# A cross-attention on one core: GpSimd computes the exponents' offset, and queues it ahead of the last scale broadcast

## The chip, the cores and the metric

The kernel runs on one core of a Trainium2 chip. A core has five engines with an instruction queue each: TensorE (PE in the profile), VectorE (DVE), ScalarE (ACT), GpSimd (POOL) and SyncE (SP), which here only issues DMAs. POOL issues DMAs too. Each queue runs in order, and queues wait for each other by semaphores. The metric is the device time in microseconds (us) of one execution of the whole program.

## The reference

The reference adds three blocks to an input x of 4 x 128 rows of 1024: a cross-attention to a context of 4 x 2048 tokens, a causal self-attention, and a feed-forward block with 4-bit weights. The change lies in the first:

```python
q, k: quantised per row of a head (64 values): q = sq * qi, k = sk * ki   # qi, ki integers
attn = softmax(q @ k.T)                     # over all 8192 tokens of the 4 batches
attn = clip(round(attn / (max(attn)/255)), 0, 255) * (max(attn)/255)
out  = attn @ v                             # v quantised per column
```

A row's largest softmax value is reached at its largest score. With s = (qi @ ki) * sk, the integer that stands for an attention value is therefore round(exp(sq * s - sq * max(s) + log 255)); the softmax's sum is needed only at the end. The offset m = -sq * max(s) + log 255, one number a row, is what this change is about.

## The kernel before

The program has stages in this order: quantised queries; keys and values of all 8192 tokens (to about 1509 us), which go through DRAM; the cross-attention; its output projection, the self-attention and the feed-forward block. The change touches the cross-attention alone.

It works through 64 units: 16 heads h, and in each head 4 row tiles t of 128 rows. A unit has 8 steps g of 1024 tokens. A loop writes out the order of the work by hand, one step after another (L876 and on; nothing reorders it), and what is issued in a step goes to the engines' queues in that order:

- scores (L746): two PE matmuls (L759) into one of two PSUM tiles sc; then DVE (L766) multiplies by the scales sk of the tokens, writes e, and keeps the chunk's largest value in a column of mx. The tile e holds half a unit (4 chunks) and has three buffers.
- maximum (L777), after the unit's eighth chunk: DVE reduces mx to its largest value (L781) and a tensor_scalar makes the offset m of it (L783): m * nsq + log 255, where nsq is -sq.
- exponentials (L789), for the unit before, at steps 0 and 4: ACT reads half a unit of e, with m as the bias, and writes int16 (tile a, three buffers).
- transposes (L803, PE and an ACT copy, 12 steps after the scores) and dma_transposes (L817, issued by SP) turn a; values (L828, PE, 18 steps after) multiplies by v.

In the last unit of a head (t = 3) each step also prepares the next head: load_keys at the first four steps, and spread_scales (L737): a POOL partition_broadcast (L739) copies one row of 1024 scales from sk_row to all 128 partitions of a tile sk. There are 8 such tiles for the 8 steps and as many buffers, so the broadcast of step g can be made only when DVE has used the same tile for the last time, in that very step. After the eighth broadcast load_rows (L731) issues, on POOL, four small DMAs that bring the row of the head after next. load_values (L726) issues the DMAs of v on POOL, four for each pair of heads.

So POOL's queue holds, for a head: eight broadcasts, four row loads and on average two loads of values; the offset m is on DVE.

Of the kernel before, what the change touches and what calls it, by code (L numbers as in the profile page):

```python
# [58 lines left out]
NSC = NK // SC  # L59
# [25 lines left out]
def tile_perceiver(  # L85
# [26 lines left out]
    nc = tc.nc  # L112
# [498 lines left out]
    def load_keys(h, c):  # L611
        kt = pools["keys"].tile([P, KC // 2], BF16, name=f"kt{h}_{c}", tag="kt", bufs=6)
        nc.sync.dma_start(out=kt, in_=k_d[c][h].rearrange("f d n -> (f d) n"))
        kts[h, c] = kt

    def tile_of_scales(h, g):
        sks_at[h, g] = pools["keys"].tile([P, SC], F32, name=f"sk{h}_{g}", tag="sk", bufs=NSC)
        return sks_at[h, g]
# [100 lines left out]
    with tc.tile_pool(name="at_s", bufs=4) as small, tc.tile_pool(  # L719
# [6 lines left out]
        def load_values(p, c):  # L726

            vqs[p, c] = at.tile([P, KT // NKC, P], F16, name=f"vq{p}_{c}", tag="vq", bufs=NKC + 1)
            nc.gpsimd.dma_start(out=vqs[p, c], in_=vq_d[p, :, ts(c, KT // NKC), :])

        def load_rows(h):  # L731

            sks_at[h] = at.tile([P, KC], F32, name=f"sk_row{h}", tag="sk_row", bufs=1)
            for c in range(NKC):
                nc.gpsimd.dma_start(out=sks_at[h][32 * c : 32 * c + 1, :], in_=sk_d[c][h : h + 1, :])

        def spread_scales(h, g):  # L737
            c, half = divmod(g, 2)
            nc.gpsimd.partition_broadcast(  # L739
                tile_of_scales(h, g), sks_at[h][32 * c : 32 * c + 1, ts(half, SC)], channels=P  # L740
            )
# [4 lines left out]
        def scores(n, g):  # L746

            h, t = units[n]
            if g == 0:
                mx = small.tile([P, NSC], F32, name="mx", tag="mx")  # L750
                state[n] = {"mx": mx, "e": [], "a": []}
            if g % (NSC // NEC) == 0:
                e = at.tile([P, EC], F32, name="e", tag="e", bufs=3)
                state[n]["e"].append(e)
            ps = sc_ps.tile([P, SC], F32, name="sc", tag="sc")

            for i in range(2):
                rows = slice(D * i, D * i + D)
                nc.tensor.matmul(  # L759
                    ps[:, ts(i, 512)],  # L760
                    lhsT=qT[rows, h, ts(t, P)],
                    rhs=kts[h, g // 2][rows, ts(g % 2, 512)],
                    start=True,
                    stop=True,
                )
            nc.vector.tensor_tensor_reduce(  # L766
                out=state[n]["e"][-1][:, ts(g % (NSC // NEC), SC)],
                in0=ps,
                in1=sks_at[h, g],
                scale=1.0,  # L770
                scalar=LOWEST,
                op0=ALU.mult,
                op1=ALU.max,
                accum_out=state[n]["mx"][:, g : g + 1],
            )

        def maximum(n):  # L777
            h, t = units[n]
            st = state[n]
            m = st["m"] = small.tile([P, 1], F32, name="m", tag="m")  # L780
            nc.vector.tensor_reduce(m, st["mx"], AX.X, ALU.max)  # L781

            nc.vector.tensor_scalar(  # L783
                m, m, nsq[:, t, h : h + 1], math.log(255.0), ALU.mult, ALU.add
            )
            if t == 0:
                sums[h] = small.tile([P, NT, NEC], F32, name="sum", tag="sum")

        def exponentials(n, c):  # L789
            h, t = units[n]  # L790
            st = state[n]
            a = at.tile([P, EC], I16, name="a", tag="a", bufs=3)
            st["a"].append(a)
            nc.scalar.activation(  # L794
                a,
                st["e"][c],
                AF.Exp,
                bias=st["m"],
                scale=sq[:, t, h : h + 1],
                accum_out=sums[h][:, t, c : c + 1],  # L800
            )

        def transposes(n, g):  # L803

            a = state[n]["a"][g // (NSC // NEC)].bitcast(F32)
            at_word = SC // 2 * (g % (NSC // NEC))
            pt = at_ps.tile([P, SC // 256, P], F32, name="a_pt", tag="a_pt")
            for i in range(SC // 256):
                nc.tensor.transpose(  # L809
                    pt[:, i, :], a[:, at_word + P * i : at_word + P * i + P], ident  # L810
                )
            aT = at.tile([P, SC // 256, P], I32, name="aT", tag="aT", bufs=4)
            nc.scalar.copy(aT, pt.bitcast(I32))
            aT = aT.bitcast(F16).rearrange("p i (q e) -> p i e q", e=2)
            state[n]["aT", g] = [aT[:, i // 2, i % 2, :] for i in range(SC // P)]

        def dma_transposes(n, c):  # L817

            at_key = c * KC % EC
            a = state[n]["a"][c * KC // EC][:, at_key : at_key + KC].bitcast(F16)  # L820
            aT = at.tile([P, KC // P, P], F16, name="aT_d", tag="aT_d", bufs=3)
            nc.sync.dma_start_transpose(out=aT, in_=a)
            for g in range(KC // SC):
                state[n]["aT", KC // SC * c + g] = [
                    aT[:, g * (SC // P) + i, :] for i in range(SC // P)
                ]
# [45 lines left out]
        def at_step(s):  # L872
            return divmod(s, NSC) if 0 <= s < n_steps else None

        with tc.manual_schedule():
            for s in range(n_steps + LAG_V):  # L876
                n, g = divmod(s, NSC)
                if s == 1:
                    for c in range(NKC):
                        load_values(0, c)  # L880
                if g == NSC // NEC and 1 <= n <= len(units):
                    dma_transposes(n - 1, DMA_KC[0])
                if g == 0 and 2 <= n <= len(units) + 1:
                    dma_transposes(n - 2, DMA_KC[1])
                if g % (NSC // NEC) == 0 and 1 <= n <= len(units):
                    exponentials(n - 1, g // (NSC // NEC))
                if n < len(units):
                    h, t = units[n]
                    scores(n, g)
                    if t == NT - 1 and h + 1 < H:  # L890

                        if g < NKC:
                            load_keys(h + 1, g)
                        spread_scales(h + 1, g)
                        if g == NSC - 1 and h + 2 < H:
                            load_rows(h + 2)
                    if g == NSC - 1:
                        maximum(n)
                at_lag = at_step(s - LAG_T)
                if at_lag and at_lag[1] * SC // KC not in DMA_KC:  # L900
                    transposes(*at_lag)
                if at_step(s - LAG_V):
                    values(*at_step(s - LAG_V))

                pair, since = divmod(s - NSC * (2 * NT - 1), NSC * 2 * NT)
                if 0 <= pair < NP - 1 and since in (0, LAG_V + 1, LAG_V + 3, LAG_V + 5):
                    load_values(pair + 1, max(0, since - LAG_V + 1) // 2)
# [290 lines left out]
    with tc.manual_schedule():  # L1198
# [11 lines left out]
        for h, (w, n) in enumerate(PARTS):  # L1210
# [20 lines left out]
            for t in range(NT):  # L1231
                g = s + GROUP * t
# [233 lines left out]
```

## Time and profile before

| | us |
|---|---|
| median of 3 runs (2888.08 to 2891.64) | 2890.35 |
| the profiled execution | 2888.83 |
| its span, first to last instruction | 2887.1 |

| engine | busy us | share of the span |
|---|---|---|
| PE | 2666.1 | 92% |
| DVE | 2411.5 | 84% |
| ACT | 1271.2 | 44% |
| POOL | 444.4 | 15% |

A line of a group of instructions reads: line of the kernel, engine, operation, tile written <- tiles read, shapes, count | busy us in all, mean ns of one | idle time of the engine just before them, with what ended most of it. A line of the timeline reads: start, duration, engine, line, operation, tiles, count, and in brackets the idle time before it and what ended it. A line for a stretch of time reads: start:end and its length, then for PE, PE's weight loads, DVE, ACT and POOL the busy us (and count), then PE's clock, the DMA engines' share and GB/s. An engine's name with a q behind it means the sequencer of that engine, which handles waits and configuration. Spans on POOL are rough.

### The profile page before, as it was taken

Reading aid. Unit: us, or ns where it says so; the run is one execution under the profiler, and the core shown is the slowest. Engines: PE = TensorE matmul, PEld = TensorE weight load, DVE = VectorE, ACT = ScalarE, POOL = GpSimd, SP = SyncE. Lnnn points to the kernel's source line nnn. Section 1 sums busy time; section 2 is a strip of 40 time slices with the busy share of each in tenths; the row PEclk is TensorE's granted clock in tenths of the full one; section 3 lists DMA queues with packets and bytes.
Section 4 is the critical chain, followed back from the end, with each engine's and each line's share of the span. In section 5 each row is a group of like instructions: output and inputs, shape, how many; then the busy total and the mean of one; then the engine's idle time right before and its main releaser. Section 6 shows DMA issues by size and latency. Waiting matters only on the chain. (4 is left out here: it accounts for less than half of the span.)

```text
span 2887.1 us, 41022 instructions
## 1 busy us (share of the span) xinstructions
PE 2666.1 (92%) x15480; PEld 2066.9 (72%) x15480; DVE 2411.5 (84%) x3946; ACT 1271.2 (44%) x1409; POOL 444.4 (15%) x596
## 2 busy tenths in 40 slices
PE   8999999999999999999987777787778899799998
PEld 3788888888888888888864555555555777688876
DVE  6899999555799998889769999999986898676674
ACT  4211111111323333333218999999993245333332
POOL 0011111000012222222112233322311000000000
PEclk9999999999999999999998999999999999899999
DMA  5555565222447777777457788878773221122222
GB/s 186 173 195 203 193 214 206 94 98 93 135 133 199 199 183 193 183 193 184 109 154 145 153 164 168 164 162 154 155 132 121 95 70 63 54 92 93 94 90 93
DMA packets 454342, 417.33 MB, mean 145 GB/s; under 512 B 357184, under 2 KB 361856, under 8 KB 454144
## 3 DMA queue, kind: packets, MB, share of 16 engines
q1 hardware_dynamic: 407648, 260.58, 37.1%
q0 software_dynamic: 45440, 153.09, 16.6%
q8 instruction: 121, 1.98, 0.3%
q10 hardware_dynamic: 1056, 1.05, 0.2%
q14 instruction: 77, 0.63, 0.1%
HBM read 224.30 MB, written 104.34 MB: 114 GB/s over the span
## 5 line engine op out<-in xcount | busy, mean ns | idle before, releaser
L342 PE MATMUL kv_a<-w_h,c_h 128*128 128x512 f32 x2048 | 806.4, 394 | 0.0
L342 PE MATMUL kv_b<-w_d,c_d 128*128 128x512 f32 x2048 | 806.0, 394 | 0.3 <-DVE c_d L157 0.3
L342 PE MATMUL kv_a<-w_l,c_l 128*128 128x512 f32 x2048 | 806.0, 394 | 0.2 <-ACT w_l L245 0.2
L766 DVE CUSTOM_DVE_ANT_0 e<-sc,sk 128x1024 f32<-128x1024 f32 x512 | 593.2, 1219 | 16.2 <-DMA k_d<-kst 8.2
L794 ACT ACTIVATE a<-e,m,sq 128x4096 int16<-128x4096 f32 x128 | 487.0, 3805 | 25.0 <-DVE m L783 24.8
L342 PEld LDWEIGHTS kv_a<-w_l,c_l 128*128 128x128 f32 x2048 | 384.8, 188 | 89.6 <-ACT w_l L245 0.6
L342 PEld LDWEIGHTS kv_b<-w_d,c_d 128*128 128x128 f32 x2048 | 384.8, 188 | 89.5 <-DVE c_d L157 0.7
L342 PEld LDWEIGHTS kv_a<-w_h,c_h 128*128 128x128 f32 x2048 | 384.9, 188 | 88.9 <-issue 0.2
L153 ACT ACTIVATE c_h<-c_raw 128x1024 fp32r<-128x1024 f32 x128 | 135.2, 1057 | 414.7 <-PE kv_a L342 405.5
L356 DVE SCALAR_TENSOR_TENSOR f<-kv_a,bkv 128x512 f32<-128x512 f32 x256 | 175.8, 687 | 163.4 <-PE kv_a L342 162.8
L759 PE MATMUL sc<-kt,qT 64*128 64x512 bf16 x1024 | 207.3, 397 | 108.9 <-DVE mx L766 104.6
L581 ACT CAST kst<-kT 128x512 bf16<-128x512 int16 x128 | 89.4, 698 | 310.1 <-DMA kT<-ki 310.0
L809 PE MATMUL a_pt<-ident,a 128*128 128x128 f32 x1024 | 176.9, 298 | 22.7 <-ACT a L794 18.0
L357 DVE SCALAR_TENSOR_TENSOR f<-kv_b,f 128x512 f32<-128x512 f32 x256 | 176.7, 690 | 20.0 <-DVE f L356 1.4
L739 POOL PARTITION_BROADCAST sk<-sk_row x120 | 142.7, 1299 | 317.9 <-DVE mx L766 317.8
L809 PEld LDWEIGHTS a_pt<-ident,a 128*128 128x128 f32 x1024 | 112.9, 146 | 88.6 <-ACT a L794 50.6
L759 PEld LDWEIGHTS <-qT 64*128 64x128 bf16 x1024 | 74.8, 93 | 137.3 <-issue 107.8
L156 DVE TENSOR_TENSOR fw_l<-fw_raw,fw_h 128x1024 fp32r<-128x1024 f32 x64 | 78.3, 1223 | 107.1 <-ACT fw_h L153 107.0
L156 DVE TENSOR_TENSOR c_l<-c_raw,c_h 128x1024 fp32r<-128x1024 f32 x128 | 155.7, 1216 | 6.0 <-ACT c_h L153 5.5
L157 DVE SCALAR_TENSOR_TENSOR c_d<-c_l,c_raw 128x1024 fp32r<-128x1024 f32 x128 | 156.3, 1221 | 2.3
L153 ACT ACTIVATE fw_h<-fw_raw 128x1024 fp32r<-128x1024 f32 x64 | 67.7, 1060 | 179.5 <-PE y_a L1369 75.2
L548 ACT CAST vq<-vi 128x1024 f16<-128x1024 int16 x64 | 66.9, 1046 | 172.2 <-DVE vi L541 123.8
(189 smaller groups left out, 4100.6 us busy)
## 6 DMA issues: line engine op xcount, KB each, us to landing
c_raw<-in_ctxT SPq DMA_DIRECT2D x128, 512.0 KB, 3.8
v_d<-f POOLq DMA_DIRECT2D x64, 512.0 KB, 3.1
vl<-v_d POOLq DMA_DIRECT2D x64, 512.0 KB, 4.2
gu_d<-w_ffn POOLq DMA_DIRECT2D x44, 512.0 KB, 3.2
fw_raw<-gu_d SPq DMA_DIRECT2D x42, 512.0 KB, 3.2
k_d<-kst POOLq DMA_DIRECT2D x128, 128.0 KB, 3.6
vq_d<-vq POOLq DMA_DIRECT2D x32, 512.0 KB, 5.1
kt<-k_d SPq DMA_DIRECT2D x64, 256.0 KB, 3.5
```

The source lines that it names most:

```text
L153: nc.scalar.mul(hi, src, 1.0 - 0.5 / UP)
L156: nc.vector.tensor_tensor(lo, src, hi, ALU.subtract)
L157: nc.vector.scalar_tensor_tensor(df, lo, -1.0 - UP, src, ALU.mult, ALU.add)
L342: nc.tensor.matmul(ps, lhsT=tokens[s][i][:, k, :], rhs=w3[s < KT][k][i][:, ts(n, 512)], start=(k == 0 and i != 1), stop=(k == NC - 1 and i ...
L356: nc.vector.scalar_tensor_tensor(f, a, 1.0 + 1.0 / UP, bias[s < KT][n], ALU.mult, ALU.add)
L357: nc.vector.scalar_tensor_tensor(f, b, -1.0 / UP, f, ALU.mult, ALU.add)
L581: nc.scalar.copy(in_order(kst, c)[:, :, :, u % 2], kTs.pop((u, n)))
L739: nc.gpsimd.partition_broadcast(tile_of_scales(h, g), sks_at[h][32 * c : 32 * c + 1, ts(half, SC)], channels=P)
L759: nc.tensor.matmul(ps[:, ts(i, 512)], lhsT=qT[rows, h, ts(t, P)], rhs=kts[h, g // 2][rows, ts(g % 2, 512)], start=True, stop=True,)
L766: nc.vector.tensor_tensor_reduce(out=state[n]["e"][-1][:, ts(g % (NSC // NEC), SC)], in0=ps, in1=sks_at[h, g], scale=1.0, scalar=LOWEST, o ...
L794: nc.scalar.activation(a, st["e"][c], AF.Exp, bias=st["m"], scale=sq[:, t, h : h + 1], accum_out=sums[h][:, t, c : c + 1],)
L809: nc.tensor.transpose(pt[:, i, :], a[:, at_word + P * i : at_word + P * i + P], ident)
```

## The change

The tensor_scalar that makes m moves from DVE to POOL. Its place in POOL's queue follows from the order of the loop: in the last unit of a head, maximum is now called ahead of the eighth spread_scales, where it was called after it and after load_rows. In other units, and in all units of the last head, it is called at the same place as before.

```diff
@@ maximum @@
-            nc.vector.tensor_scalar(
+            nc.gpsimd.tensor_scalar(
                 m, m, nsq[:, t, h : h + 1], math.log(255.0), ALU.mult, ALU.add
             )
@@ the loop over steps @@
                         if g < NKC:
                             load_keys(h + 1, g)
+
+                        if g == NSC - 1:
+                            maximum(n)
                         spread_scales(h + 1, g)
                         if g == NSC - 1 and h + 2 < H:
                             load_rows(h + 2)
-                    if g == NSC - 1:
+                    elif g == NSC - 1:
                         maximum(n)
```

The `elif` belongs to `if t == NT - 1 and h + 1 < H`. The offset, its inputs and its readers stay as they are.

## Prediction

> **What bounds the kernel now.** I read the busy table by slices first, then the stage the diff touches, then single instructions there. The touched stage is the cross attention, 1509 to 2140 us. Its window and groups (busy us, mean ns, idle before it and what ended that):
>
> ```profile
> 1509.00:2140.00 631.00, 491.52 (x5878) 339.96 (x5877) 615.74 (x1191) 595.23 (x495) 188.22 (x212) 0.96 0.80 158
> ```
> ```profile
> L766 DVE CUSTOM_DVE_ANT_0 e<-sc,sk 128x1024 f32<-128x1024 f32 x512 | 593.2, 1219 | 16.2 <-DMA k_d<-kst 8.2 <-PE sc L759 6.9 <-ACT a L794 0.8
> L783 DVE TENSOR_SCALAR m<-m,nsq 128x1 f32<-128x1 f32 x64 | 13.7, 214 | 2.3
> L794 ACT ACTIVATE a<-e,m,sq 128x4096 int16<-128x4096 f32 x127 | 483.2, 3805 | 25.0 <-DVE m L783 24.8
> ```
>
> DVE is busy 615.7 of 631 us and ACT 595.2; POOL only 188. DVE bounds, with ACT close behind, and POOL looks free. The end of one unit, on DVE and then ACT:
>
> ```profile
> 1790.39 1.22 DVE L766 CUSTOM_DVE_ANT_0 e<-sc,sk 128x1024 f32<-128x1024 f32 x1
> ...
> 1791.65 0.16 DVE L781 TENSOR_REDUCE m<-mx 128x1 f32<-128x8 f32 x1
> 1791.85 0.21 DVE L783 TENSOR_SCALAR m<-m,nsq 128x1 f32<-128x1 f32 x1
> 1791.99 1.23 DVE L766 CUSTOM_DVE_ANT_0 e<-sc,sk 128x1024 f32<-128x1024 f32 x1
> ```
> ```profile
> 1792.10 3.81 ACT L794 ACTIVATE a<-e,m,sq 128x4096 int16<-128x4096 f32 x1
> ```
>
> A unit starts on DVE every 9.60 us (1791.99, 1801.60, 1811.19); chunks are 1.144 us apart. ACT's exponentials start as soon as m is there. POOL around two changes of head:
>
> ```profile
> 1783.70 9.42 POOL L739 PARTITION_BROADCAST sk<-sk_row  x8 [13.93 <-DVE mx L766]
> 1793.41 1.96 POOL L735 DMA_DIRECT2D sk_row<-sk_d  x4 [0.29 <-POOL sk L739]
> 1823.16 1.29 POOL L739 PARTITION_BROADCAST sk<-sk_row  x1 [27.80 <-DVE mx L766]
> 1824.29 0.57 POOL L729 DMA_DIRECT2D vq<-vq_d  x1
> 1824.88 8.26 POOL L739 PARTITION_BROADCAST sk<-sk_row  x7
> ```
>
> The eight scale tiles of a head have one buffer each, so the broadcasts for the next head run in the last unit of this head, one behind each chunk, and end a moment before the next head needs them: 9.4 us of work in 9.6. So POOL, free on average, has no slack just there.
>
> **The decisive resource.** The order of the changed program's instructions shows more on POOL than 64 small operations: each time POOL goes from a broadcast (L739) to the tensor_scalar (L783) or back, an extra pool-configuration instruction stands before it, 31 at L783 and 30 at L739. The kernel before has three of this kind. In the trace (name, duration ns, first and last start us):
>
> ```profile
> L974 POOL TENSOR_TENSOR x<-x,sv_bp x8: 1257/1263/2247, 2173.9 to 2184.3; 128x512 f32<-128x512 f32 x8
> ...
> L974 POOLq MODIFY_POOL_CONFIG  x2: 12/12/12, 2165.7 to 2165.7; - x2
> L974 POOLq EVENT_SEMAPHORE  x1: 17/17/17, 2172.7 to 2172.7; - x1
> ```
> ```profile
> L523 POOLq EVENT_SEMAPHORE  x3: 17/1038/11950, 795.7 to 796.9; - x3
> L523 POOLq MODIFY_POOL_CONFIG  x2: 37/37/37, 796.2 to 796.2; - x2
> L523 POOL PARTITION_ALL_REDUCE vall<-vmax x1: 3247/3247/3247, 809.0 to 809.0; - x1
> ```
> ```profile
> masks.py:199 POOLq MODIFY_POOL_CONFIG  x2: 12/12/12, 1.1 to 1.2; - x2
> ```
>
> At L974 (from broadcasts back to ordinary arithmetic) the sequencer takes 12 ns, but the first operation starts 8.2 us later. Its transfer of x, issued at 2167.0, landed 5.7 us on, at 2172.7, and the wait passed then; the remaining 1.2 us has no releaser. At a later L974 operation (wait passed 2275.2, start 2275.3) that step takes 0.1 us. So I read 8.2 us as the switch. The other direction (L523) is bounded only from above: 796.2 to 809.0, 12.8 us, the wait for DVE covers it. The first one (masks.py, 1.2 to its operation at 1.2) costs nothing, but is no change from broadcasts.
>
> [...] broadcasts report 1299 ns, but eight take 9.42 us, so the spacing is 1.16.
>
> **The change part by part.**
> Removed: 64 tensor_scalars on DVE. One occupies the slot from 1791.85 to 1791.99, 0.14 us, up to 0.34 if the next chunk overlaps the reduce as well. ACT's floor per unit is two halves of 4.74 (1787.24 less 1782.50), 9.48, against 9.60; so at most 0.12 x 64 = 7.7 us.
> Added: 64 on POOL. Not shown; between 0.1 (POOL's 128x1 memset) and 1.3 us (its 128x512 operations); I take 0.3 with the hand-over: DVE's 0.21 plus 0.1. L783 also waits for the reduce, and behind it in POOL's queue stand broadcasts and loads.
> Moved: L783 of a head's last unit stands ahead of the eighth broadcast, so POOL's program for a head change is: m(t=2), switch, seven broadcasts, switch, m(t=3), switch, broadcast 8, four row loads, switch, m(t=0). It is serial. With R for a switch, counted from the reduce of t=2:
> three m: 0.9; seven broadcasts 8.26; the eighth 1.30; four row loads 0.29 + 1.96; vq load 0.57 in every second head, 0.3. Sum 13.0 + 4R until m(t=0) is there.
> From there: first half of the exponentials 3.80 + 0.1. The e tiles have three buffers, so chunks 5 to 8 of unit t=1 wait for that half; from the fifth chunk to the next unit is 5.02 (1796.58 to 1801.60); then unit t=2 up to its reduce, 9.44. Sum 18.4. Head period 31.4 + 4R.
> Before: mean of the 15 head periods (first L783 to first L783) is 40.0.
> R = 8.2: 64.2, so +24.2 a head, x15 changes of head = +363. Why DVE can't run ahead: with m(t=3) at 0.3 + 8.2 + 8.26 + 8.2 + 0.3 = 25.3 instead of 9.85, chunks 5 to 8 of t=0 wait for an e tile, the eighth waits for its scales (25.3 + 8.2 + 1.3 = 34.8 instead of 17.8), and m(t=0) comes at 45.8. The first switch, before unit 0, hides behind that unit. Units t=1 and t=2 need no switch; in every second head m(t=1) now queues behind two vq loads that wait for PE, but those went out at 1844.5 and 1847.5 and its reduce ends at 1850.5, so 3 us cover it (and the third load, now behind m(t=1), is needed only a unit later). Against this: the last head change has no row loads (-2.3), and L974's own switch goes (-1.2, the part without cover). PE and the DMA transposes on SP follow late and add nothing of their own.
> Profiled execution 2888.8 + 360 = 3249; the median 2890.35 stands 1.5 above it, so 3250.
> Both ends of R: [...] At 8.2 one way and 12.8 the other (mean 10.5) 73.4, +33.4 x 15 = 501, 3388.
>
> **Rivals.**
> *A switch costs next to nothing* (0.1, as at masks.py). Then POOL's chain stays inside DVE's time and only the removal counts: 2890 - 8 = 2882, faster. For it: the 12 ns record, and that 7.0 of the 8.2 us at L974 lie under a transfer's wait. Against: the 1.2 us without a releaser. It decides below about R = 1: m(t=3) is then at 1.5 (first broadcast after its chunk) + 8.26 + 1 + 0.3 = 11.1, 1.2 late, of which 0.6 is slack (half ends 1795.9, fifth chunk 1796.58); the 0.6 left equals four removals of 0.14.
> *The load begins only at the first call and lasts 1.2 us.* m(t=3) is 1.4 late, 0.8 after slack: +12 less 8, about 2895, the same within error.
> *Switches are slower beside this stage's transfers* (DMA share 0.80, against 0.78 in the L974 gap, hence not my choice): R = 12.8 both ways gives 82.6 a head, 3530.
> *The wait on DVE's handover alone*: 64 later starts of ACT by some 0.2 us would fit in the 0.6 us slack; nothing.
>
> **How the numbers follow.** [...] The cheap cases: 0.05, split 0.03 faster, 0.02 same. Likeliest 3250; [...] 0.2% (some 6 us) is about what a measurement of this kernel can tell.
>
> **What would show it.** Per head change four configuration pairs at L783 and L739, each followed by an idle POOL of about 8 us; ACT waiting for POOL's m some 24 us a head, near 360 in all, against 24.8; DVE's L766 idle rising from 16 by about as much; unit starts near 64 us per four; PE's and DVE's busy times unchanged, the stages before 1509 and after 2160 unchanged but for the shift. It is wrong if the gap behind a configuration is near 1 us, or if the loads overlap the broadcasts in front of them.

## The result and the profile after

The changed kernel takes 3233.09 us (median of 4 runs, 3227.76 to 3234.56) where the kernel before takes 2889.22 in the same sessions: a ratio of 1.1181, 95% interval 1.1163 to 1.1199, slower. The forecast was 3250. The profiled execution took 3231.92 us, its span is 3230.1, and 339 of the 343 us between the two spans lie in the 15 head periods: they average 62.6 us against 40.0.

The cross attention now runs from 1509 to about 2487 us. Its window, and the groups that answer to those of before:

```profile
1509.00:2487.00 978.00, 556.22 (x5876) 376.34 (x5876) 614.60 (x1129) 594.85 (x494) 211.97 (x274) 0.75 0.52 102
```
```profile
L766 DVE CUSTOM_DVE_ANT_0 e<-sc,sk 128x1024 f32<-128x1024 f32 x512 | 601.9, 1221 | 367.0 <-ACT a L794 289.0 <-PE sc L759 64.9 <-DMA kt<-k_d 11.9
L783 POOL TENSOR_SCALAR m<-m,nsq 128x1 f32<-128x1 f32 x64 | 16.5, 258 | 517.8 <-DVE m L781 290.0 <-issue 210.5 <-DVE mx L766 17.2
L794 ACT ACTIVATE a<-e,m,sq 128x4096 int16<-128x4096 f32 x127 | 483.1, 3804 | 379.5 <-POOL m L783 379.4
```

DVE and ACT have no more work: they are busy 614.6 us (615.7 before) and 594.9 (595.2), POOL only 212, in a stage that is 347 us longer. PE's busy time grew from 491.5 to 556.2 us for the same instructions, at a lower granted clock (0.75 for 0.96). What grew most is waiting: ACT for m, from 24.8 to 379.4 us, and DVE for ACT to free an e tile, 289.0 us. POOL itself is idle, and 210.5 us of its idle time in front of the offsets has no releaser ("issue").

POOL through one change of head (t=2's m to the next t=0's m):

```profile
1864.35 0.27 POOL L783 TENSOR_SCALAR m<-m,nsq 128x1 f32<-128x1 f32 x1 [10.18 <-DVE m L781]
1871.83 1.30 POOL L739 PARTITION_BROADCAST sk<-sk_row  x1 [7.21 <-DVE mx L766]
1872.98 0.74 POOL L729 DMA_DIRECT2D vq<-vq_d  x1
1873.77 7.09 POOL L739 PARTITION_BROADCAST sk<-sk_row  x6
1887.87 0.25 POOL L783 TENSOR_SCALAR m<-m,nsq 128x1 f32<-128x1 f32 x1 [7.00 <-issue]
1894.15 1.31 POOL L739 PARTITION_BROADCAST sk<-sk_row  x1 [6.03 <-issue]
1895.75 2.16 POOL L735 DMA_DIRECT2D sk_row<-sk_d  x4 [0.29 <-POOL sk L739]
1905.15 0.25 POOL L783 TENSOR_SCALAR m<-m,nsq 128x1 f32<-128x1 f32 x1 [7.23 <-issue]
```

Every time POOL goes from the tensor_scalar to the broadcasts or back, there is a gap of 6 to 8 us in front of the new operation: four gaps here, of 6.0 to 7.2 us, 27.5 of 40.8 us. (The first is put down to DVE's mx, but the chunk that this broadcast needs had been done for some 6 us.) The configurations behind the gaps are in the line of the offset and of the broadcasts; these are 31 and 30 switches of two records each, whose own durations tell nothing of it:

```profile
L783 POOLq MODIFY_POOL_CONFIG  x62: 37/127/129, 1518.8 to 2459.3; - x62
L739 POOLq MODIFY_POOL_CONFIG  x60: 11/11/11, 1548.9 to 2452.4; - x60
```

From a configuration's second record to the operation, the median over the stage is 7.28 us towards the tensor_scalar and 5.94 towards the broadcast.

### The profile page after: what moved, and what is told of

The parts are those of the page before. It is cut to its first block, busy times and chain, and to the rows that moved or that the text cites. A ratio compares the mean times of both kernels' runs of the same rounds, so it can differ in the third digit from the quotient of the medians.

```text
span 3230.1 us, 41263 instructions
## 1 busy us (share of the span) xinstructions
PE 2728.4 (84%) x15480; PEld 2100.4 (65%) x15480; DVE 2409.8 (75%) x3882; ACT 1271.0 (39%) x1409; POOL 467.6 (14%) x660
## 4 chain that ended last, share of the span: by engine, by line
PE 68%; DVE 14%; issue 11%; POOL 4%; ACT 1%; DMA 1%; SPq 0%; POOLq 0%; DVEq 0%; ACTq 0%
PE kv_a L342 29%; PE kv_b L342 14%; DVE e L766 9%; POOL sk L739 3%; PE a_pt L809 3%; PE acc_a L1027 3%; PE y_a L1372 2%; PE gate_a L163 2%; PE up_a L163 2%; PE sc L759 2%; PE q_ps L291 2%; PE av L835 1%; PE y_b L1372 1%; PE acc_b L1027 1%; PE gate_b L163 1%
## 5 line engine op out<-in xcount | busy, mean ns | idle before, releaser
L766 DVE CUSTOM_DVE_ANT_0 e<-sc,sk 128x1024 f32<-128x1024 f32 x512 | 601.9, 1221 | 367.0 <-ACT a L794 289.0
L794 ACT ACTIVATE a<-e,m,sq 128x4096 int16<-128x4096 f32 x128 | 486.9, 3804 | 379.5 <-POOL m L783 379.4
L809 PE MATMUL a_pt<-ident,a 128*128 128x128 f32 x1024 | 206.9, 335 | 334.7 <-ACT a L794 334.5
L809 PEld LDWEIGHTS a_pt<-ident,a 128*128 128x128 f32 x1024 | 132.2, 166 | 408.2 <-ACT a L794 353.9
L759 PE MATMUL sc<-kt,qT 64*128 64x512 bf16 x1024 | 228.7, 440 | 81.8 <-DVE mx L766 77.7
L759 PEld LDWEIGHTS <-qT 64*128 64x128 bf16 x1024 | 66.9, 95 | 116.4 <-issue 82.1
L835 PEld LDWEIGHTS <-aT 128*128 128x128 f16 x2048 | 83.3, 104 | 88.2 <-issue 75.1
```

Of the source, the lines that this page charges most:

```text
L759: nc.tensor.matmul(ps[:, ts(i, 512)], lhsT=qT[rows, h, ts(t, P)], rhs=kts[h, g // 2][rows, ts(g % 2, 512)], start=True, stop=True,)
L766: nc.vector.tensor_tensor_reduce(out=state[n]["e"][-1][:, ts(g % (NSC // NEC), SC)], in0=ps, in1=sks_at[h, g], scale=1.0, scalar=LOWEST, o ...
L794: nc.scalar.activation(a, st["e"][c], AF.Exp, bias=st["m"], scale=sq[:, t, h : h + 1], accum_out=sums[h][:, t, c : c + 1],)
L809: nc.tensor.transpose(pt[:, i, :], a[:, at_word + P * i : at_word + P * i + P], ident)
```

## Experiments

All times are medians beside runs of the kernel before on the same chip. The edits are shown against the changed kernel; those that leave part of the tiles on DVE, against the kernel before.

**The order alone.** The changed kernel with the offset back on DVE, so that only the call's place differs from before.

```diff
-            nc.gpsimd.tensor_scalar(
+            nc.vector.tensor_scalar(
                 m, m, nsq[:, t, h : h + 1], math.log(255.0), ALU.mult, ALU.add
```

> The order of the changed kernel, but the offset is made on DVE as before; POOL has no switch of its configuration in the stage. Theory (the switches on POOL's serial chain are the whole cost): 2889 within 6 us, period of a head 40.0. Rival (the new place in the order costs something by itself): above 2900.

Measured: 2892.16 against 2891.72, ratio 1.0002 (0.9993 to 1.0010). The place in the order costs nothing while the offset is on DVE. (POOL's own queue is as before here; its order with the offset in it is tested by the last experiment.)

**The engine alone.** POOL makes the offset, but maximum is called where it was, behind the broadcast and the row loads.

```diff
-                        if g == NSC - 1:
-                            maximum(n)
                         spread_scales(h + 1, g)
 ...
-                    elif g == NSC - 1:
+                    if g == NSC - 1:
                         maximum(n)
```

> The offset on POOL, but called at its old place, behind the eighth broadcast and the row loads: 2 switches a head instead of 4. Theory (what counts is POOL's serial chain until an offset that ACT waits for): until m(t=3) 0.44 + 7.0 + eight broadcasts 9.85 + row loads 2.46 + 7.36 + 0.25 = 27.4, then 3.83 + 6.80 to the end of t=0, 10.2 and 11.0 for t=1 and t=2: 59.2 a head, 2889 + 15 x 19.2 = 3177. Rival (each switch has its price wherever it stands, 344 / 61 = 5.6 us): 31 switches, 3064.

Measured: 3159.70, ratio 1.0916 (1.0896 to 1.0937); a head takes 58.2 us where 59.2 was worked out. With half the switches, 268 of 344 us remain. That is far from the 3064 of a fixed price for each switch: the three offsets of t=0 to t=2 then need no switch, but m(t=3) stands behind two switches, eight broadcasts and the row loads, and the whole core waits for it.

**The switches with nobody waiting for them.** DVE makes the offset; POOL, at the place of the changed kernel, computes a value that is not used. It reads nsq alone, so it does not wait for a reduce either.

```diff
+            nc.vector.tensor_scalar(
+                m, m, nsq[:, t, h : h + 1], math.log(255.0), ALU.mult, ALU.add
+            )
+            idle = small.tile([P, 1], F32, name="idle", tag="idle", bufs=1)
             nc.gpsimd.tensor_scalar(
-                m, m, nsq[:, t, h : h + 1], math.log(255.0), ALU.mult, ALU.add
+                idle, nsq[:, t, h : h + 1], nsq[:, t, h : h + 1], 1.0, ALU.mult, ALU.add
             )
```

> The offset on DVE, and at the place where the changed kernel has it on POOL a tensor_scalar on POOL whose result nobody reads: the same 61 switches, with no offset behind them. Theory: only the eighth broadcast is late, at 1.5 + 8.3 + 7.2 + 0.25 + 6.1 + 1.3 = 24.6 instead of 17.8 after the reduce of t=2, so +7 to +8.5 a head, 2994 to 3017; the switches around t=0 to t=2 are hidden. Rival (a price for each switch, or POOL's loads slow the other engines): as the changed kernel, 3233.

Measured: 3017.36, ratio 1.0428 (1.0412 to 1.0443), at the upper end of the forecast; 48.4 us a head. The same 61 switches cost 126 us instead of 344. DVE's groups in this kernel:

```profile
L766 DVE CUSTOM_DVE_ANT_0 e<-sc,sk 128x1024 f32<-128x1024 f32 x512 | 597.0, 1220 | 142.9 <-POOL sk L739 104.7 <-PE sc L759 24.8 <-DMA kt<-k_d 12.4
```

DVE now waits for the eighth broadcast alone, 104.7 us or 7.0 a head (6.8 was worked out). The switches don't slow the other engines by themselves: an operation of L766 takes 1220 ns (1219 before), one of ACT's exponentials 3804 (3805). Two switches, 13.3 us, stand in front of the eighth broadcast; what is paid is the part of them that is left when the time until this broadcast is due has been used up.

**Two more switches a head.**

```diff
 ...
                         if g == NSC - 1:
                             maximum(n)
+                            nc.gpsimd.load_library(all_libraries[1])
+                            nc.gpsimd.load_library(all_libraries[0])
                         spread_scales(h + 1, g)
```

Library 1 is the configuration that the broadcasts use here, library 0 that of the tensor_scalar; a third switch, back to 1, follows as in the changed kernel.

> The changed kernel with two more switches a head, to the broadcasts' configuration and back with no operation between them, behind the offset of t=3. Theory (a switch is carried out when POOL's queue reaches it, some 6.1 and 7.2 us, and POOL's chain sets the time): +13.3 a head, 3233 + 15 x 13.3 = 3433. Rival (the load begins only with the first operation after it, so that a switch without operation is free): 3233.

Measured: 3425.34, ratio 1.1845 (1.1828 to 1.1862), 534 us above its own runs of the kernel before where the changed kernel is 344 above: 190 us more, 12.6 a head. POOL around the place, and the configurations there:

```profile
1721.58 0.25 POOL L784 TENSOR_SCALAR m<-m,nsq 128x1 f32<-128x1 f32 x1 [7.04 <-issue]
1740.81 1.31 POOL L740 PARTITION_BROADCAST sk<-sk_row  x1 [18.98 <-issue]
```
```profile
L898 POOLq MODIFY_POOL_CONFIG  x2: 11/11/11, 1722.1 to 1722.2; - x2
L899 POOLq MODIFY_POOL_CONFIG  x2: 7/7/7, 1727.8 to 1727.8; - x2
L740 POOLq MODIFY_POOL_CONFIG  x2: 7/7/7, 1735.1 to 1735.1; - x2
```

Three switches in a row leave 18.98 us where one left 6.03: 6.5 us for each of the added ones, though no operation stands between them. Each configuration is held up by the one in front of it, by 5.6 and then 7.3 us. So here a switch is carried out when the queue reaches it, not when an operation first needs it: the two added ones cost 190 us. That removes the rival in which the load begins at the first call; that it lasts 1.2 us was refuted by the gaps already.

**POOL for three tiles of four.** DVE makes the offset for t=3, POOL for t=0 to t=2; the order of before.

```diff
-            nc.vector.tensor_scalar(
+            engine = nc.gpsimd if t in (0, 1, 2) else nc.vector
+            engine.tensor_scalar(
```

> The offset on POOL for t=0 to t=2, on DVE for t=3; 31 switches, as many as with the old place on POOL for all tiles. Theory: broadcasts and row loads end at 19.8 after the reduce of t=2, the switch back at 27.2, so m(t=0) is there at 27.4 (due 19.6); then 3.83 + 6.80 + 11.0: 49.0 a head, 2889 + 15 x 9.0 = 3024. Rival (a price for each switch): 3064, and the same time as the other kernel with 31 switches.

Measured: 3024.01, ratio 1.0467 (1.0452 to 1.0482), and 48.2 us a head where 49.0 was worked out; that the sum agrees so closely is chance: the heads give 12 us less than worked out, and other places make up for it, the last head with 5.6. As many switches as with the engine alone, and 135 us above the kernel before instead of 268: what they stand in front of sets the price.

**POOL for t=1 and t=2.** The same edit with `(1, 2)`; both switches of a head should be hidden.

> The offset on POOL for t=1 and t=2 of a head alone, on DVE for t=0 and t=3; 31 switches. Theory: both switches of a head are hidden: broadcasts start at 0.44 + 7.0 and the eighth ends at 17.3 (17.9 with a vq load) where 17.8 is due, row loads and the switch back end at 27.2 where the offset of t=1 is due at 28.8. DVE is relieved of 32 operations, 0.12 to 0.2 us each: 2883 to 2890. Rival (a price for each switch): 3064.

Measured: 2928.47, ratio 1.0123 (1.0106 to 1.0140): a miss by 38 us. From the third on, every second head took 45 us, the others 39.1 to 41.6. POOL in one of the long ones, and its configuration there:

```profile
1694.25 0.54 POOL L729 DMA_DIRECT2D vq<-vq_d  x1 [2.58 <-PE av L836]
1702.92 0.25 POOL L784 TENSOR_SCALAR m<-m,nsq 128x1 f32<-128x1 f32 x1 [8.13 <-DVE mx L766]
```
```profile
L784 POOLq MODIFY_POOL_CONFIG  x2: 37/37/37, 1694.9 to 1694.9; - x2
```

The switch is placed right before the operation that needs it, and so behind the two loads of values, which wait for PE until 1694; only then does it begin, and m(t=1) is 8.1 us behind the second of them. In the other heads it begins some 9 us ahead of the offset and is hidden by the wait for DVE. I had looked at these loads as a wait of their own that 3 us covered, not as something that holds back a switch.

**The same, with the switch ahead of these loads.**

```diff
 ...
                         if g == NSC - 1 and h + 2 < H:
                             load_rows(h + 2)
+                        if g == NSC - 1:
+                            nc.gpsimd.load_library(all_libraries[0])
```

> As the kernel with POOL's offset for t=1 and t=2 alone (2928), but the switch back to arithmetic is issued right behind the row loads, ahead of the two loads of values that wait for PE in every second head. Theory (the miss of that kernel was the switch queued behind these loads): the +6 us in every second head go, the other heads have 39.1 to 40.1 us now where before has 39.5 to 40.4; 2880 to 2890. Rival (a switch costs something else, wherever it is hidden): still about 2928.

Measured: 2892.68 against 2891.79, ratio 1.0007 (0.9996 to 1.0017). With the same number of switches, m(t=1) now comes 0.4 to 0.5 us after its reduce in every head, where it came 5.6 to 6.6 us after it in the long ones: the switch behind the loads caused the 6 us, and 31 switches that are hidden cost nothing that shows. The gain for DVE doesn't show either, and the time is above the forecast. In the profiled execution, which at 2900.75 is the slowest of the 14, units t=1 take 9.39 us instead of 9.60, but some of the others grow, one by 5 us in which DVE mostly waits for PE; over all runs the sum is no change.

**One configuration for both operations.** The changed kernel's order, with the offset as two tensor_tensors (log255 is a column of that value) and one library that serves these and the broadcasts. It is loaded once, in the second step of the first unit.

```diff
 ...
-            nc.gpsimd.tensor_scalar(
-                m, m, nsq[:, t, h : h + 1], math.log(255.0), ALU.mult, ALU.add
-            )
+            nc.gpsimd.tensor_tensor(m, m, nsq[:, t, h : h + 1], ALU.mult)
+            nc.gpsimd.tensor_tensor(m, m, log255, ALU.add)
 ...
                     for c in range(NKC):
                         load_values(0, c)
+                    nc.gpsimd.load_library(all_libraries[10])
```

> The changed kernel's order and engine, but the offset as two POOL tensor_tensors (times nsq, plus a column of log 255), with one configuration, set once before the first unit, that serves them and the broadcasts: no switch in the stage. Theory: POOL's chain fits again; m comes some 0.5 us later after its reduce than on DVE, inside the 0.6 us of slack; DVE is relieved of 64 operations: 2880 to 2892. Rival (arithmetic on POOL, its handover, or its place ahead of the eighth broadcast is what costs): above 3000.

Measured: 2900.22 against 2889.11, ratio 1.0040 (1.0026 to 1.0054). With the switches gone, 333 of the 344 us are gone, with POOL still making all offsets ahead of the eighth broadcast. But the 11 us left are outside the forecast: POOL's version is a little slower than DVE's, not faster. POOL and ACT at a change of head:

```profile
1668.33 7.09 POOL L740 PARTITION_BROADCAST sk<-sk_row  x6
1675.51 0.19 POOL L784 TENSOR_TENSOR m<-m,nsq 128x1 f32<-128x1 f32 x1
1675.77 0.19 POOL L785 TENSOR_TENSOR m<-m,log 128x1 f32<-128x1 f32 x1
```
```profile
L794 ACT ACTIVATE a<-e,m,sq 128x4096 int16<-128x4096 f32 x128 | 486.9, 3804 | 44.1 <-POOL m L785 43.4
```

m is there 0.60 us after its reduce where DVE needs 0.25, and for t=3, behind six broadcasts with a value load among them, 1.1 us (the reduce ended at 1674.86). ACT's wait for m is 43.4 us instead of 24.8, and the unit after a change of head takes 10.16 us instead of 9.61, the first unit's successor 13.6 instead of 11.5 (the one switch is in front of it). What a one-operation offset without any switch would give was not tried.

No version ran faster than the kernel before.

## Why the prediction was right, and where its terms were off

**The mechanism held at each step.** The bound moved from DVE to POOL's queue, as a serial chain of four switches, eight broadcasts, row loads and three offsets; ACT waits for m, and DVE for the e tile that ACT holds. The order alone (1.0002) and the one configuration (1.0040) show that neither the place, nor the engine without switches, is behind the 344 us; two more switches (+190) show that each added one on the chain is paid in full; the unused results (+126) and the tiles on POOL show that the number of switches is not the price, but what stands behind them.

**The rivals.** A switch of next to nothing fell by the gaps (5.94 and 7.28 us), a load at the first call by the two added switches. Slower switches beside this stage's transfers did not come: in the changed kernel they take 5.6 to 7.7 us, less than the 8.2 us at L974 (the first one's 9.6 us end with a wait for DVE). But this kernel is a poor test of them, since its stalls thin the transfers out: the DMA engines' share in the stage fell from 0.80 to 0.52, and in six switches towards the tensor_scalar (between 1817 and 1968 us), of 7.0 to 7.4 us each, it was 0 to 0.53. Towards the broadcasts, the 15 switches behind m(t=2), at a share of 0.80 to 1.06, took 5.9 to 7.6 us (median 6.5), and the 15 behind m(t=3), at 0.15 to 0.21, 5.6 to 6.0 (5.8). With POOL for t=1 and t=2, the seven such switches behind loads of values ran at a share of 0.75 or more and took 7.8 to 8.7 us. So a switch may well be slower beside transfers, and 8.2 us right at L974, where the share is 0.78; no run changes the transfers alone.

**The size was right partly by luck.** The terms of one head, measured as the mean of 13 changes of head, beside the forecast:

| term | forecast, us | measured, us |
|---|---|---|
| four switches (POOL's idle time at each) | 32.8 | 27.6 (7.0, 7.1, 6.1, 7.4) |
| POOL's own work: offsets, broadcasts, row and value loads | 13.0 | 13.4 |
| m to the end of the first exponentials | 3.9 | 3.8 |
| fifth chunk of t=1 to the next unit | 5.0 | 6.8 |
| unit t=2 to its reduce | 9.4 | 11.3 |
| head period | 64.2 | 62.9 |

The switches were mis-sized by 5.2 us a head: 7.0 of the 8.2 us at L974 lie under a transfer's wait, which gave an upper bound where I took a value; that a switch takes more than the remaining 1.2 us was not shown by the trace of before, it was my estimate. What that one start waited for stays open. Two terms were too small by 3.6 and hid it: with 27.6 us for the switches, the prediction's own sum gives 59.0 a head and some 3170 in all, 60 us short. Unit t=2 was priced as a plain unit of 9.6 less its tail, though the trace of before has it at 10.6 to 11.6, since the previous head's normalisation (L847 to L858) falls into it; its mean up to the reduce was 10.9 there. And the fifth to eighth chunks were priced at full PE speed. PE after a stall, in the changed kernel:

```profile
1909.38 1.12 PE L809 MATMUL a_pt<-ident,a 128*128 128x128 f32 x4 [6.53 <-ACT a L794]
...
1915.13 0.66 PE L809 MATMUL a_pt<-ident,a 128*128 128x128 f32 x4
```

Four transposes take 1.12 us right after 6.5 us of idling and 0.66 six microseconds later. The scores of the next chunks stand behind these in PE's queue (the next ones start at 1910.86 and 1912.87), and DVE pauses 0.9 and 0.8 us for sc.

**What would show it.** ACT's wait (379 for 360), DVE's idle time (367) and the head period came as said. POOL's gaps were 6 to 7 us, not 8. PE's busy time was said to stay; it rose from 2666.1 to 2728.4, by the slow stretches.

**The handover** was said to fit in 0.6 us of slack. In plain units it does; with one configuration for both operations it cost 11 us in all, most of it where POOL has broadcasts in front of the offset and where the only switch stands.

## What to carry to other kernels

An engine that is idle on average can still have no slack at one place (POOL, busy 188 of the stage's 631 us, was busy 9.4 of 9.6 us at a change of head): look at what stands in its queue there, and at how the new work changes what the queue must do between its instructions. On GpSimd, look for configurations between operations of different kinds and count them in program order. Here each change between partition_broadcast and tensor_scalar was worth 6 to 7 us in the changed kernel (medians 5.94 and 7.28), up to 8.7 with POOL for t=1 and t=2; the records of the configuration itself (11 to 129 ns) don't show it. What it costs depends on what is queued behind it, and on what it is queued behind: 31 switches cost 268, 135, 37 or 1 us. A few 128x1 operations taken off the busiest engine were worth nothing here when the result then reached the next engine later: with m 0.60 instead of 0.25 us after its reduce, and one switch in the stage, the ratio was 1.0040.

## What the runs showed that I had not expected

- A switch on POOL depends on its direction: 5.94 us (median of 30) towards partition_broadcast, 7.28 (of 31) towards tensor_scalar, in the changed kernel. The switches added with no operation between them took 5.75 and 7.33 (medians of 15).
- TensorE's mean granted clock in the stage fell from 0.96 to 0.75, in a stage where PE idles 32 times for 4 to 15 us. At the stall above, the granted clock had fallen to 0.50 at 1903.9, 1.0 us after PE's last matmul; it was 0.50 until 1914.1, 4.7 us after PE's restart, and 1.00 from there. The four transposes take 1.12 us at 0.50 and 0.66 at 1.00. The recorded changes of the clock lie 3.41 us or a multiple of it apart. In the 3.41 us before this fall (1900.46 to 1903.87) PE was busy 1.56 us. In the 3.41 us before each of the stage's 41 falls to 0.50 PE was busy 0 to 63% of the time (0 in four of them), and before each of its 42 returns 99% or more. One stall at a change of head so cost about 1.8 us more than its length (6.8 for 5.0 us in the table).
- Two tensor_tensors of 128x1 on POOL take 0.19 us each and follow 0.26 us apart; a tensor_scalar of that size takes 0.26, not much more than DVE's 0.21. The hand-over costs more: in plain units m is there 0.43 us after DVE's reduce where DVE's own tensor_scalar needs 0.25.
